# First pair of a feed-forward quantized inside the cross attention, and a table of zeros filled there instead of at the start

## The chip, the cores and the metric

The kernel runs on one core of a Trainium2 chip. A core has TensorE (PE, with its weight loads listed as PEld), VectorE (DVE), ScalarE (ACT), GpSimd (POOL) and SyncE (SP); each has its own queue of instructions, worked off in order, and meets the others through semaphores. DMAs are issued from the queues of SP, ACT and POOL. The metric is the device time of one execution in microseconds (us), the median of several runs.

## The reference

The computation is a decoder of two layers on `x` of 16 sequences x 128 tokens x 512 features, with a layernorm after every residual sum. Cut to what matters:

```python
# layer 0
x = ln(x + ssm(x))            # selective scan over 4 x 1024 tokens, 16 states per feature
x = ln(x + cross(x, ctx))     # 16 heads of 128, rope and rms norm on q and k
x = ln(x + ffn(x))
# layer 1
x = ln(x + bit_attention(x)); x = ln(x + gated_cross(x, ctx)); x = ln(x + moe(x))

def ffn(x):                   # ternary weights, 8-bit activations
    n = (x - mean(x)) / sqrt(var(x) + 1e-8)
    s = 127 / max(abs(n), -1)
    q = clip(round(s * n), -128, 127) / s
    return (silu(q @ sign(W_g).T) * (q @ sign(W_u).T)) @ sign(W_d).T
```

The mixture of experts routes each token to 8 of 64 experts. The kernel collects the rows of each group of experts in buckets in device memory, which have to hold zeros before rows are written to them.

## The kernel before, in words

Five stages run one after the other: `stage_ssm` (0 to about 623 us of the profiled span), `stage_xattn` (to about 1641), `stage_ffn` (to about 1938), `stage_attention` and `stage_moe`. The sixteen `x` tiles of 128 tokens x 512 features stay in on-chip memory throughout.

A tile scheduler orders the work. It takes the program's instructions in the order in which they are written as priorities, models their durations, and may place an instruction on its engine's queue earlier or later than it is written, as far as data and buffers allow. An instruction that is written in one stage can therefore run in another. Once compiled, each queue is fixed. A DMA goes out on one of eight lanes in turn, and its issue waits on the issuing queue until the DMA before it on that lane has landed.

*The scan stage.* Eight pairs of sequences, 16 states each, give 128 units. For each unit ACT computes decays (`h`, L234 and L236), SP loads the row `BC` broadcast to all partitions (L243), POOL multiplies (`dBx`, L245), DVE runs a scan (L254 or L258), and PE sums over states into `py` (L267). In between, a plan written by hand steps three side jobs: the projection of the next pair, the output of the last pair (L182 to L201, ending in the normalization L200), and the keys and values of a later cross attention (`keys_values`, L203 to L225), whose tiles go to device memory by DMAs that ACT issues (`x_k`, L215; `x_v`, L223). After the last state ACT copies the sums `y` (L272).

*The cross attention.* For each sequence `project` loads the transposed context `cT` (SP, L473), makes queries, keys and values (L483), and applies rope (L450 to L460) with tables of sines that `SinTables` builds on DVE (L349 to L368). Units of two heads then go through a pipeline: scores (L555), maximum (L561), exponential (L568), norm (L574, L575), transposes (L583, L586), outputs (`ao` L595, `aT` L600, `po` L606) and the sum into `x` (L609). A list `running` holds jobs that `advance` steps once for each step of the pipeline; it begins with `clear_rows` (L394 to L402), which writes 16 rows of `results` and, by 96 DMAs of 388 KB, the buckets, all from a table `zeros` in device memory. That table is filled at the very start of the program: one `x` tile is set to zero, and two POOL DMAs (L1700, L1701) copy it.

*The feed-forward.* `load_ffn_weights` loads weights and takes their signs on ACT (L659 for gate and up, L669 for down, tiles `w`). The weights share five slots of on-chip memory, so that a load or a sign waits until the slot's last reader is done. Pairs of sequences are then prepared: normalized (`xn`, L72), quantized (`qs`, `q_t`, `q_q`, L680 to L691), and transposed on PE (`ptq`, L701) into `q_T` (L703). The loop does, for each quarter `h` of the hidden features, the products `pg` and `pu` (L755), silu and product (`sg`, L758 on ACT, L759 on DVE), four transposes, a split in a high and a low part (L764, L765), and the product `po` (L769). Beside it run side jobs for the next stage, stepped from the second pair on by this line and its body:

```python
if n and h >= 2:
    next(ahead, None)
```

The jobs are the scales and ternary weights of the bit attention (`load_bit_weights`, with sums `bw_tot` at L807) and the mask of the gated attention (`load_gated_masks`: `anyk` L834, `mb` L837 and L839). The first pair is prepared before the loop, in one go:

```python
for _ in prepare(states[0]):
    pass
```

Of the kernel before, what the change touches and what calls it, by code (L numbers as in the profile page):

```python
# [10 lines left out]
F32 = mybir.dt.float32  # L11
BF16 = mybir.dt.bfloat16
# [3 lines left out]
AF = mybir.ActivationFunctionType  # L16
ALU = mybir.AluOpType
AX = mybir.AxisListType
PSUM = bass.MemoryType.PSUM

P = 128
NB = 16
D = 512
KC = D // P
NT = NB * P
MAGIC = 12582912.0
# [48 lines left out]
def stage_ssm(k):  # L75
# [6 lines left out]
    nc, tc, a = k.nc, k.tc, k.args  # L82
    NS, BQ = 16, 2
    TQ = BQ * P
    with ExitStack() as ctx:
        cst = ctx.enter_context(tc.tile_pool(name="s1c", bufs=1))
# [160 lines left out]
        def scan(u):  # L247
            st, n = units[u]
            h = st.h[n]
            hf, df = h.rearrange("p c b t -> p (c b t)"), st.dBx[n].rearrange("p c t -> p (c t)")  # L250
            Cn = st.BC[n][:, 1].unsqueeze(1).to_broadcast([P, KC, TQ])
            if n % 8 in (1, 4, 6):
                hC = wk.tile([P, KC, TQ], F32, tag="hs", name="hs")
                nc.vector.tensor_tensor_scan(hC.rearrange("p c t -> p (c t)"), hf, df, 0.0, ALU.mult, ALU.add)  # L254
                nc.gpsimd.tensor_tensor(hC, hC, Cn, ALU.mult)
            else:
                hC = wk.tile([P, KC, TQ], F32, tag="hC", name="hC", bufs=3)
                nc.vector.tensor_tensor_scan(hf, hf, df, 0.0, ALU.mult, ALU.add)  # L258
                nc.vector.tensor_tensor(hC, h.rearrange("p c b t -> p c (b t)"), Cn, ALU.mult)
            st.hC[n] = hC  # L260
# [30 lines left out]
        for u, (st, n) in enumerate(units):  # L291
            p = u // NS
            if n == 0:
                if p + 1 < NP:
                    nxt = project(states[p + 1], load_x(p + 1))
                for i in range(BQ):
                    nc.sync.dma_start(k.x[p * BQ + i], a["x"][p * BQ + i])
                if p == 2:
                    load_xattn_weights(k, 0)
            if u + 1 < len(units):  # L300
                decays(u + 1)
            if u + 2 < len(units):
                terms(u + 2)
            scan(u)
            for what in plan[n].strip("-") if u else "":
                next({"k": kv, "o": late, "n": nxt}[what], None)
            if u:
                add(u - 1)
            if u == 2:
                load_kv()  # L310
            if n == 0 and p:
                late = output(p - 1, states[p - 1].y)
# [78 lines left out]
            nc.sync.dma_start(k.wo[i], a["xa_woT"][i * 1024 : (i + 1) * 1024].rearrange("(h p) e -> p h e", p=P))  # L391


def clear_rows(k):  # L394

    for h in range(2):
        for bucket, result in zip(k.bucket[h], k.results[h]):
            k.nc.sync.dma_start(result[0:1], k.zeros[0:1, 0:D])
            for j in range(Moe.TILES):
                k.nc.sync.dma_start(bucket[j * P : (j + 1) * P], k.zeros)  # L400
                yield


def stage_xattn(k):
# [9 lines left out]
    with ExitStack() as ctx:  # L414
# [175 lines left out]
        def outputs(st, g):  # L590
# [17 lines left out]
            if g == G - 1:  # L608
                nc.vector.tensor_tensor(k.x[st.b], st.po, k.x[st.b], ALU.add)  # L609
                yield  # L610
                if st.b % 2:
                    xs = k.x[st.b - 1 : st.b + 1]
                    layernorm(k, xs, xs)
                    yield

        def advance():
            for job in list(running):
                if next(job, running) is running:
                    running.remove(job)

        units = [(b, g, i) for b in range(NB) for g in range(G) for i in range(2)]
        running = [clear_rows(k)]
        for t in range(-12, len(units) + 4):
            for lag, what in ((3, turn), (2, norm), (1, exps), (0, top), (-1, scores)):
                if not 0 <= t - lag < len(units):
                    continue
                b, g, i = units[t - lag]
                st = state[b]
                if what is scores and (g, i) == (0, 0):
                    st.b, st.sc, st.mx, st.pr, st.sm, st.pTs = b, {}, {}, {}, {}, {}  # L630
                what(st, g, i)
                if what is turn and i == 1:
                    running.append(outputs(st, g))
            b, r = divmod(t + 11, U)
            if r == 0 and b < NB:
                running.append(project(b))
            b, r = divmod(t + 15, U)
            if t == -12 or r == 0 and b > 0 and b < NB and b % 4 == 0:
                running.append(angles(max(b, 0) // 4))
            advance()  # L640
# [29 lines left out]
        k.fd.append(fd.rearrange("p (h e) -> p h e", h=8))  # L670


def quantize(k, ins, floor=None):


    nc, n = k.nc, len(ins)
    s = k.small.tile([P, n], F32, tag=f"qs{n}", name="qs")
    step = k.small.tile([P, n], F32, tag=f"qst{n}", name="qst")
    for i, x in enumerate(ins):
        nc.vector.tensor_reduce(s[:, i : i + 1], x, AX.X, ALU.max, apply_absolute_value=True)  # L680
    if floor is not None:
        nc.vector.tensor_scalar(s, s, floor, None, ALU.max)
    nc.vector.reciprocal(s, s)
    nc.vector.tensor_scalar(s, s, 127.0, None, ALU.mult)
    nc.vector.reciprocal(step, s)
    outs = []
    for i, x in enumerate(ins):
        t = k.wk.tile([P, D], F32, tag="q_t", name="q_t")
        q = k.wk.tile([P, D], BF16, tag="q_q", name="q_q")
        nc.vector.tensor_scalar(t, x, s[:, i : i + 1], MAGIC, ALU.mult, ALU.add)  # L690
        nc.scalar.activation(q, t, AF.Identity, bias=k.nmagic)  # L691
        outs.append(q)
    return outs, step


def transpose_q(k, pool, q):

    nc = k.nc
    pt = pool.tile([P, KC, P], BF16, tag="pp", name="ptq")
    for c in range(KC):  # L700
        nc.tensor.transpose(pt[:, c], q[:, c * P : (c + 1) * P], k.identb)  # L701
    qT = k.wk.tile([P, KC, P], BF16, tag="q_T", name="q_T")
    nc.scalar.copy(qT, pt)  # L703
    return qT


def stage_ffn(k):
# [2 lines left out]
    nc, tc = k.nc, k.tc  # L710
    HB = 4
    with ExitStack() as ctx:
        k.wk = wk = ctx.enter_context(tc.tile_pool(name="s3w", bufs=3))
        pg = ctx.enter_context(tc.tile_pool(name="s3g", bufs=2, space=PSUM))
        pp = ctx.enter_context(tc.tile_pool(name="s3p", bufs=2, space=PSUM))
        po_ = ctx.enter_context(tc.tile_pool(name="s3o", bufs=1, space=PSUM))
# [2 lines left out]
        ahead = chain(load_bit_weights(k, raws, po_), load_gated_masks(k, raws))  # L719

        def prepare(st):

            xn = [wk.tile([P, D], F32, tag="xn", name="xn") for _ in st.xs]
            layernorm(k, st.xs, xn, 1e-8)
            yield
            qs, st.step = quantize(k, xn)
            yield
            st.qT = []
            for q in qs:
                st.qT.append(transpose_q(k, po_, q))  # L730
                yield

        def finish(st):
            layernorm(k, st.xs, st.xs)
# [1 line left out]

        states = []
        for b0 in range(0, NB, 2):
            st = Ctx()
            st.xs = k.x[b0 : b0 + 2]  # L740
            states.append(st)
        for _ in prepare(states[0]):
            pass
        late = iter(())
        for n, sn in enumerate(states):
            nxt = prepare(states[n + 1]) if n + 1 < len(states) else iter(())
# [36 lines left out]
def load_bit_weights(k, raws, psum):  # L783
# [20 lines left out]
    views = [raw[:, :, 0:512], rawo, raw[:, :, 512:640], raw[:, :, 640:768]]  # L804
    tot = k.small.tile([P, 4], F32, tag="bw_tot", name="bw_tot", bufs=1)
    for i, w in enumerate(views):
        nc.vector.tensor_reduce(tot[:, i : i + 1], w, AX.XY, ALU.add, apply_absolute_value=True)  # L807
        yield
    pt = psum.tile([P, 4], F32, tag="pp", name="ptw")
    nc.tensor.matmul(pt, ones, tot, start=True, stop=True)  # L810
# [7 lines left out]
    outs = [wb[:, :, 0:512], wb[:, :, 768:1280], wb[:, :, 512:640], wb[:, :, 640:768]]  # L818
    for i, (w, o) in enumerate(zip(views, outs)):
        nc.vector.tensor_scalar(w, w, rsw[:, i : i + 1], MAGIC, ALU.mult, ALU.add)  # L820
        nc.vector.tensor_scalar(w, w, MAGIC, 1.0, ALU.subtract, ALU.min)
        nc.vector.tensor_scalar(o, w, -1.0, None, ALU.max)
        yield


def load_gated_masks(k, raws):


    nc, a, pool = k.nc, k.args, k.bit_pool
    m8 = raws.tile([P, NB, P], U8, name="m8")  # L830
    nc.sync.dma_start(m8, a["mask"].rearrange("b t -> (b t)").partition_broadcast(P).rearrange("p (b t) -> p b t", b=NB))
    yield
    k.gated_any = pool.tile([P, NB], F32, name="anyk")
    nc.vector.tensor_reduce(k.gated_any, m8, AX.X, ALU.max)  # L834
    yield
    k.gated_mask = mb = pool.tile([P, NB, P], BF16, name="mb")
    nc.vector.tensor_scalar(mb, m8, 1e30, -1e30, ALU.mult, ALU.add)  # L837
    yield
    nc.vector.tensor_tensor(mb, mb, k.gated_any.unsqueeze(2).to_broadcast([P, NB, P]), ALU.mult)  # L839
    yield  # L840


# [829 lines left out]
def decoder(ctx: ExitStack, tc: tile.TileContext, args):  # L1672
# [22 lines left out]
    k.zeros = dram.tile([P, Moe.ROW], F32, name="zeros")  # L1695
    k.moe, k.to_route, k.moe_ctx = None, [], ctx.enter_context(ExitStack())
    k.x = [const.tile([P, D], F32, name=f"x{b}") for b in range(NB)]
    zero = k.x[NB - 1]
    nc.gpsimd.memset(zero, 0.0)
    nc.gpsimd.dma_start(k.zeros[:, 0:D], zero)  # L1700
    nc.gpsimd.dma_start(k.zeros[:, D:], zero[:, 0 : Moe.ROW - D])  # L1701
    wctx = ctx.enter_context(ExitStack())
    wpool = wctx.enter_context(tc.tile_pool(name="weights", bufs=5, side="right"))
    k.wslot = lambda dt=F32: wpool.tile([P, 8192 if dt == BF16 else 4096], dt, tag="w", name="w")
    nc.scalar.preload_act_table_set("natural_log_exp_and_others")
    actx = ctx.enter_context(ExitStack())
    for stage in STAGES:
        if stage is stage_ffn:
            k.bit_pool = actx.enter_context(tc.tile_pool(name="bit", bufs=1))
        if stage is stage_attention:  # L1710
            wctx.close()
            k.gated_pool = actx.enter_context(tc.tile_pool(name="gated", bufs=1))
        if stage is stage_moe:
            actx.close()
        stage(k)
# [77 lines left out]
```

## Time and profile before

| what | value |
|---|---|
| median of 3 runs | 3377.56 us (3376.58 to 3380.5) |
| profiled execution | 3382.4 us |
| its span | 3380.6 us |
| mean granted clock of TensorE | 0.965 |
| PE busy | 3153.0 us, 93% |
| DVE, ACT, POOL busy | 1876.7, 1379.5, 1389.5 us |
| moved by DMA | 317.28 MB, mean 94 GB/s |

The page of the profile has the busy time of each engine, the span cut into 40 slices with the busy share of each engine in tenths, the DMA queues, and the costliest groups of instructions. In a line of a timeline stand the start, the duration, the engine, the line of the code, the operation, outputs and inputs, the number of instructions taken together, and in brackets how long the engine had been idle before and what released it. "ACTq" and "SPq" are the sequencers of these engines, which issue DMAs. Buffer numbers are left out of names. A mean over the span hides that the stages have different limits, so the stretches around the change are read one by one.

### The profile page before, as it was taken

What the parts mean: (1) busy time and instruction counts of PE and PEld (TensorE: products, weight loads), DVE (VectorE), ACT (ScalarE), POOL (GpSimd) and SP (SyncE); (2) the same over time, 40 slices, a digit from 0 to 9 for tenths busy, and PEclk for the clock granted to TensorE, in tenths of its full rate; (3) what the DMA queues carried; (4) which work ended last, traced back from release to release, by engine and by line L of the source; (5) the groups of instructions that cost most, each with busy time, mean ns of one, the idle gap of its engine ahead of it and who ended that gap; (6) DMA issues with size and microseconds to landing.
All of it is one profiled execution on the core that took longest, in us unless ns stands there. A gap on an engine that the chain in (4) does not pass through costs nothing. (4 is left out here: it accounts for less than half of the span.)

```text
span 3380.6 us, 38522 instructions
## 1 busy us (share of the span) xinstructions
PE 3153.0 (93%) x12894; PEld 1813.6 (54%) x12944; DVE 1876.7 (56%) x4202; ACT 1379.5 (41%) x3299; POOL 1389.5 (41%) x1198
## 2 busy tenths in 40 slices
PE   6888999899999999999799989998989999989998
PEld 3444444355555555555466555665655566556665
DVE  5877888456556556455576669765643232222223
ACT  4655655133333233234333379865643232112221
POOL 6967887133323333332000066325624454233331
PEclk8999999899999999999899989999999999999999
DMA  6887332200000000002200010013335665445441
GB/s 230 261 259 223 98 88 69 68 7 4 7 4 4 7 4 4 7 1 94 91 1 1 17 47 1 11 57 148 137 133 175 201 233 189 163 156 172 163 158 65
DMA packets 161553, 317.28 MB, mean 94 GB/s; under 512 B 19113, under 2 KB 82089, under 8 KB 158276
## 3 DMA queue, kind: packets, MB, share of 16 engines
q1 hardware_dynamic: 123012, 215.83, 20.8%
q0 software_dynamic: 19328, 64.56, 5.5%
q10 hardware_dynamic: 19008, 34.35, 2.7%
q8 instruction: 105, 1.72, 0.2%
q14 instruction: 100, 0.82, 0.1%
HBM read 238.80 MB, written 129.04 MB: 109 GB/s over the span
## 5 line engine op out<-in xcount | busy, mean ns | idle before, releaser
L245 POOL TENSOR_TENSOR dBx<-dtx,BC 128x1024 f32<-128x1024 f32 x128 | 301.2, 2373 | 44.8 <-DVE h L258 35.1
L1529 PE MATMUL pg<-gu,xgT 128*128 128x352 f32 x784 | 301.7, 467 | 0.0
L1529 PE MATMUL pu<-gu,xgT 128*128 128x352 f32 x784 | 299.6, 464 | 0.0
L1546 PE MATMUL y<-dn,aT 128*128 128x512 f32 x588 | 268.3, 592 | 0.0
L1533 DVE SCALAR_TENSOR_TENSOR act<-pu,row,act 128x352 f32<-128x352 f32 x98 | 57.1, 583 | 376.3 <-PE pu L1529 317.9
L575 POOL TENSOR_TENSOR pr<-pr,sm 128x512 f32<-128x512 f32 x128 | 134.7, 1053 | 289.6 <-DVE sm L574 244.2
L236 ACT ACTIVATE h<-dt,negA 128x254 f32<-128x254 f32 x512 | 239.8, 474 | 14.9 <-DVE dt L178 2.1
L1572 POOL TENSOR_TENSOR x<-got,x 128x512 f32<-128x512 f32 x120 | 152.2, 1274 | 226.4 <-DMA got<-results,gidx 225.2
L606 PE MATMUL po<-w,aT 128*128 128x512 f32 x512 | 232.2, 597 | 1.1 <-DVE aT L600 1.1
L483 PE MATMUL pq<-w,xT 128*128 128x512 f32 x512 | 228.9, 594 | 0.0
L1565 POOL DMA_INDIRECT got<-results,gidx x120 | 116.2, 968 | 268.9 <-DMA results<-yo 216.1
L460 POOL TENSOR_TENSOR m<-m,m 128x512 f32<-128x512 f32 x96 | 121.6, 1267 | 247.0 <-DVE m L455 247.0
L258 DVE TENSOR_TENSOR_SCAN h<-h,dBx 128x1024 f32<-128x1024 f32 x80 | 183.0, 2294 | 71.0 <-ACT h L236 48.7
L568 ACT ACTIVATE pr<-sc,mx,sf 128x256 f32<-128x256 f32 x256 | 142.8, 562 | 187.0 <-DVE mx L561 176.1
L267 PE MATMUL py<-hC,ident 128*128 128x512 f32 x320 | 164.6, 643 | 49.1 <-ACT y L272 49.1
L1529 PEld LDWEIGHTS pu<-gu,xgT 128*128 128x128 f32 x784 | 151.2, 193 | 85.1 <-issue 4.2
L1529 PEld LDWEIGHTS pg<-gu,xgT 128*128 128x128 f32 x784 | 144.1, 194 | 64.7 <-issue 3.0
L1532 ACT ACTIVATE act<-pg 128x352 f32<-128x352 f32 x98 | 45.5, 464 | 318.6 <-PE pg L1529 248.9
L1546 PEld LDWEIGHTS y<-dn,aT 128*128 128x128 f32 x588 | 104.1, 190 | 100.8 <-issue 94.2
L1521 ACT COPY xgT<-ptx 128x512 f32<-128x512 f32 x98 | 57.5, 587 | 233.9 <-PE ptx L375 209.6
L483 PEld LDWEIGHTS pq<-w,xT 128*128 128x128 f32 x512 | 93.5, 190 | 102.0 <-issue 99.0
L606 PEld LDWEIGHTS po<-w,aT 128*128 128x128 f32 x512 | 95.4, 191 | 96.9 <-issue 92.9
(363 smaller groups left out, 6808.3 us busy)
## 6 DMA issues: line engine op xcount, KB each, us to landing
bucket<-zeros SPq DMA_DIRECT2D x96, 388.0 KB
row<-bucket SPq DMA_DIRECT2D x90, 388.0 KB
BC<-bcd SPq DMA_DIRECT2D x128, 256.0 KB
results<-yo ACTq DMA_DIRECT2D x90, 256.0 KB
gu<-in_moe_guT SPq DMA_DIRECT2D x16, 1408.0 KB
cT<-in_ctxT SPq DMA_DIRECT2D x32, 256.0 KB
dn<-in_moe_downT SPq DMA_DIRECT2D x16, 512.0 KB
rows<-r_row SPq DMA_DIRECT2D x16, 388.0 KB
```

The source lines that it names most:

```text
L236: nc.scalar.activation(h[:, c, :, 1:], st.dt[:, c].rearrange("p (b t) -> p b t", b=BQ)[:, :, 1:], AF.Exp, scale=negA[:, c, n : n + 1])
L245: nc.gpsimd.tensor_tensor(dBx, st.dtx, BC[:, 0].unsqueeze(1).to_broadcast([P, KC, TQ]), ALU.mult)
L258: nc.vector.tensor_tensor_scan(hf, hf, df, 0.0, ALU.mult, ALU.add)
L267: nc.tensor.matmul(st.py[c], k.ident, st.hC[n][:, 2 * c : 2 * c + 2], start=n == 0, stop=n == NS - 1)
L460: nc.gpsimd.tensor_tensor(m1, m1, m2, ALU.add)
L483: nc.tensor.matmul(ps, src[:, c], w[c], start=c == 0, stop=c == KC - 1)
L568: nc.scalar.activation(pr[:, j], st.sc[g, i][:, j], AF.Exp, scale=st.sf[:, h : h + 1], bias=st.mx[g, i][:, j : j + 1], accum_out=sm[:, j : ...
L575: nc.gpsimd.tensor_tensor(pr, pr, sm.unsqueeze(2).to_broadcast([P, 2, 2 * P]), ALU.mult)
L606: nc.tensor.matmul(st.po, aT[:, j], k.wo[h // 8][:, h % 8], start=h == 0, stop=h == G * J - 1)
L1529: nc.tensor.matmul(ps, u.xT[:, c], gu[:, c, lo : lo + I], start=c == 0, stop=c == KC - 1)
L1546: self.nc.tensor.matmul(u.y, u.aT[:, c], u.w[1][:, c], start=c == 0, stop=c == 2)
L1572: nc.gpsimd.tensor_tensor(k.x[b], got, k.x[b], ALU.add)
```

## The change

Four edits go together.

1. The table of zeros is no longer filled at the start of the program. `clear_rows` takes a pool of the cross attention, sets a tile of 128 x 97 elements to zero there, and fills the table by eight DMAs on SP, each of 97 columns (388 bytes a row). The clears read that table, as before.
2. The feed-forward's first pair is prepared by a job `prepare_first` in the list `running` of the cross attention, appended four units before the last. It uses tiles of the cross attention: `xn` in the buffers `m1`, `q_t` in `m2`, `q_q` in `sq`, the transposes in the PSUM buffers `pt`; only `q_T` has buffers of its own, in a new pool `early`. Preparation itself is one generator, `prepare_ffn`, for the first pair and for the later ones.
3. The DVE instructions of the side jobs in the feed-forward are wrapped in `keep_in_program_order`, so that the scheduler doesn't move them against the instructions written around them.
4. In the scan stage, `add(u - 1)` comes ahead of the plan's step for the first state of a pair, and after it for the others.

```diff
@@ stage_ssm
             scan(u)
+            if u and not n:
+                add(u - 1)
             for what in plan[n].strip("-") if u else "":
                 next({"k": kv, "o": late, "n": nxt}[what], None)
-            if u:
+            if n:
                 add(u - 1)
@@
-def clear_rows(k):
-
+def clear_rows(k, pool):
+
+    n = Moe.ROW // 8
+    zero = pool.tile([P, n], F32, name="zero")
+    k.nc.gpsimd.memset(zero, 0.0)
+    for i in range(8):
+        k.nc.sync.dma_start(k.zeros[:, i * n : (i + 1) * n], zero)
+    yield
     for h in range(2):
         for bucket, result in zip(k.bucket[h], k.results[h]):
             k.nc.sync.dma_start(result[0:1], k.zeros[0:1, 0:D])
@@ stage_xattn
+        def prepare_first():
+
+            homes = {"xn": (wk, "m1", 4), "q_t": (wk, "m2", 2), "q_q": (wk, "sq", 2), "pt": (ppt, "pt", 2), "q_T": (k.early, "q_T0", 2)}
+            st = k.ffn_first = Ctx()
+            st.xs = k.x[0:2]
+
+            def new(what, shape, dt):
+                pool, tag, bufs = homes[what]
+                return pool.tile(shape, dt, tag=tag, name=what, bufs=bufs)
+
+            return prepare_ffn(k, st, new)
...
-        running = [clear_rows(k)]
+        running = [clear_rows(k, cst)]
...
+            if t == len(units) - 4:
+                running.append(prepare_first())
@@
-def quantize(k, ins, floor=None):
...
-def transpose_q(k, pool, q):
...
+def prepare_ffn(k, st, new):
+
+    nc = k.nc
+    xn = [new("xn", [P, D], F32) for _ in st.xs]
+    layernorm(k, st.xs, xn, 1e-8)
+    yield
+    s = k.small.tile([P, 2], F32, tag="qs2", name="qs")
+    st.step = k.small.tile([P, 2], F32, tag="qst2", name="qst")
+    for i, x in enumerate(xn):
         nc.vector.tensor_reduce(s[:, i : i + 1], x, AX.X, ALU.max, apply_absolute_value=True)
     nc.vector.reciprocal(s, s)
     nc.vector.tensor_scalar(s, s, 127.0, None, ALU.mult)
+    nc.vector.reciprocal(st.step, s)
+    qs = []
+    for i, x in enumerate(xn):
+        t = new("q_t", [P, D], F32)
+        qs.append(new("q_q", [P, D], BF16))
         nc.vector.tensor_scalar(t, x, s[:, i : i + 1], MAGIC, ALU.mult, ALU.add)
+        nc.scalar.activation(qs[i], t, AF.Identity, bias=k.nmagic)
+    yield
+    st.qT = []
+    for q in qs:
+        pt = new("pt", [P, KC, P], BF16)
+        for c in range(KC):
+            nc.tensor.transpose(pt[:, c], q[:, c * P : (c + 1) * P], k.identb)
+        st.qT.append(new("q_T", [P, KC, P], BF16))
+        nc.scalar.copy(st.qT[-1], pt)
+        yield
@@ stage_ffn
-            st = Ctx()
+            st = Ctx() if b0 else k.ffn_first
             st.xs = k.x[b0 : b0 + 2]
             states.append(st)
-        for _ in prepare(states[0]):
-            pass
@@ load_bit_weights, load_gated_masks
-        nc.vector.tensor_reduce(tot[:, i : i + 1], w, AX.XY, ALU.add, apply_absolute_value=True)
+        k.tc.keep_in_program_order(nc.vector.tensor_reduce(tot[:, i : i + 1], w, AX.XY, ALU.add, apply_absolute_value=True))
...
-    nc.vector.tensor_reduce(k.gated_any, m8, AX.X, ALU.max)
+    k.tc.keep_in_program_order(nc.vector.tensor_reduce(k.gated_any, m8, AX.X, ALU.max))
...
@@ decoder
-    zero = k.x[NB - 1]
-    nc.gpsimd.memset(zero, 0.0)
-    nc.gpsimd.dma_start(k.zeros[:, 0:D], zero)
-    nc.gpsimd.dma_start(k.zeros[:, D:], zero[:, 0 : Moe.ROW - D])
...
+        if stage is stage_xattn:
+            k.early = actx.enter_context(tc.tile_pool(name="early", bufs=1))
```

## The prediction

> **What bounds the kernel now.** I read the page first: TensorE is the busiest engine, in nearly every slice, while the DMA engines are full only in the first sixth of the span. That sixth is where the 96 large clears (37 MB) run.
>
> ```profile
> PE 3153.0 (93%) x12894; PEld 1813.6 (54%) x12944; DVE 1876.7 (56%) x4202; ACT 1379.5 (41%) x3299; POOL 1389.5 (41%) x1198
> PE   6888999899999999999799989998989999989998
> DMA  6887332200000000002200010013335665445441
> bucket<-zeros SPq DMA_DIRECT2D x96, 388.0 KB
> ```
>
> Next, the table of windows over the stretches that the change touches (columns: stretch; length; PE, PEld, DVE, ACT, POOL busy; clock; DMA share; GB/s). The cross attention (640 to 900) keeps PE busy for 255 of 260 us with idle queues; the feed-forward from 1700 is at 235.88 of 238. Between them lie 21 us in which PE does 1.2 us of work and DVE 20.8.
>
> ```profile
> 640.00:900.00 260.00, 255.25 (x829) 135.56 (x828) 153.18 (x405) 89.61 (x211) 97.39 (x107) 0.99 0.02 6
> 1641.00:1662.00 21.00, 1.21 (x9) 0.98 (x10) 20.83 (x65) 5.93 (x8) 1.26 (x4) 0.59 0.43 140
> 1662.00:1700.00 38.00, 37.68 (x175) 22.67 (x178) 17.68 (x28) 14.54 (x23) 0.00 (x0) 0.96 0.00 1
> 1700.00:1938.00 238.00, 235.88 (x1142) 145.53 (x1161) 157.90 (x428) 82.84 (x135) 0.00 (x0) 1.00 0.00 1
> ```
>
> **The scan stage, where the clears leave.** The clears are called in the cross attention, but the scheduler puts them on SP from 97 to 343 us, between the loads of BC. In the DVE timeline the first scans of the eight pairs start at 36.3, 100.4, 161.9, 239.2, 317.2, 387.3, 458.3 and 529.5 us: the pairs from the fifth on, clear of clears, take 70.2, 70.9 and 71.3 us (mean 70.8), the third and fourth 77.4 and 77.9. The ACT timeline shows why: in the third pair the store of the keys (L215) waits on ACT's own queue from 171.2 to 179.4 for a load of BC that stands behind clears. The normalization L200 behind it then runs at 179.7. In a quiet pair the store issues at once. PE's sum `py` waits for ACT's copy of `y`, behind all this: 9.78 us against 4.95.
>
> ```profile
> 170.66 0.58 ACT L214 COPY kt<-pk 128x512 f32<-128x512 f32 x1
> 179.36 0.33 ACTq L215 DMA_DIRECT2D x_k<-kt  x1
> 179.74 1.52 ACT L200 ACTIVATE x<-x,s_sh,rs_y 128x512 f32<-128x512 f32 x2 [8.50 <-DMA BC<-bcd]
> 190.66 2.08 PE L267 MATMUL py<-hC,ident 128*128 128x512 f32 x2 [9.78 <-ACT y L272]
> ...
> 396.14 0.58 ACT L214 COPY kt<-pk 128x512 f32<-128x512 f32 x1
> 396.75 0.33 ACTq L215 DMA_DIRECT2D x_k<-kt  x1
> 403.24 1.52 ACT L200 ACTIVATE x<-x,s_sh,rs_y 128x512 f32<-128x512 f32 x2 [6.52 <-DVE s_sh L198]
> 411.31 2.08 PE L267 MATMUL py<-hC,ident 128*128 128x512 f32 x2 [4.95 <-ACT y L272]
> ```
>
> The change fills the table of zeros only in the cross attention, so no clear can run earlier. The compiled order of PE, ACT, DVE and POOL in this stage stays the same; SP loses 112 clears. Gain by difference to the quiet pairs: 77.4 - 70.8 = 6.6 and 77.9 - 70.8 = 7.1. In the second pair a value copy waits 1.76 us for the key store (113.8 us); I take 2.0 with what follows it (0 to 2.5). At the start a memset and two POOL DMAs of 0.39 MB leave the queues ahead of the first matmul at 12.3 us, of some 3.5 MB queued there: 0.5 (0 to 1.3). Sum -16.2, bounds -8 (only half of the difference is the clears') to -18.
>
> **The cross attention, where the clears arrive.** SP now has eight table DMAs, 16 small clears and 96 large ones. In SP's new order the eight stand ahead of the first `cT`, each after the second waiting on the queue for an earlier load (wo, norm weights, positions) to land, so `cT` comes some 4 to 5 us later than for its present matmul at 633.4. Its result isn't needed at once: the next product `pv` started at 645.5, released by the rope on DVE, which waited for the sine tables (POOL's `tk0c`, 644.0). The cover is about 5 us after the 6 us of matmul; without it each us late is one us. I take +0.5, bounds -1 to +3.
> The table is now written in rows of 388 bytes. By the nearest rate in the trace, 246 GB/s in the window of 97 to 343, 0.39 MB take 1.6 us. The Trainium skill ("DMA: Bandwidth & Descriptors", Specifications) says that below 512 bytes a transfer misses line rate through read-modify-write; nothing in this trace isolates it. If it doubles the write, an estimate of mine from that page, everything behind is 1.6 us later: inside the cover, so +0.5 by the one, up to +2 by the other. I take the trace.
> The large clears then share SP with `cT`: 9 stand before the second, and 17, 34, 68 and 96 in all before the third to sixth. Those are needed at 672, 712, 774, 838 and 899 us; from 637 that leaves 3.9, 4.4, 4.0, 3.0 and 2.7 us for each. Between 97 and 343 us they took 246/96 = 2.56 us each beside other traffic; at 246 GB/s alone 1.6. So 0, bounds 0 to +5. No instruction leaves PE here, so no gain.
>
> **The feed-forward's start.** These are PE, ACT and DVE lines in turn:
>
> ```profile
> 1637.31 3.70 PE L606 MATMUL po<-w,aT 128*128 128x512 f32 x8 [0.78 <-DVE aT L600]
> 1659.98 0.61 PE L701 MATMUL ptq<-identb,q_q 128*128 128x128 bf16 x4 [18.97 <-ACT q_q L691]
> 1668.87 1.19 PE L769 MATMUL po<-w,hi 128*128 128x512 f32 x4
> ...
> 1641.80 3.89 ACT L669 ACTIVATE w<-w 128x1024 fp32r<-128x1024 f32 x4 [9.25 <-DMA w<-in_ff_wdT]
> 1662.49 1.28 ACT L758 ACT_TABLE_LOAD   x1
> ...
> 1648.15 2.29 DVE L807 TENSOR_REDUCE bw_tot<-l_raw 128x1 f32<-128x2048 f32 x1
> 1658.58 0.86 DVE L690 TENSOR_SCALAR q_t<-xn,qs 128x512 f32<-128x512 f32 x2
> 1665.58 0.74 DVE L759 SCALAR_TENSOR_TENSOR sg<-pu,qst,sg 128x512 f32<-128x512 f32 x1
> ```
>
> PE waits 18.97 us for the first pair's quantization, which DVE reaches late because 9.4 us of side jobs (sums of the next stage's weights: 2.29 + 0.68 + 2.28 + 0.68; mask: 2.28 + 1.22) lie in its way, and a 2.29 us one ahead of the first `sg`. In the new order the pair is quantized inside the cross attention and the side jobs stand after the twelfth `sg`.
> What is late next? ACT: the signs of the last down weights start when these landed and the last `po` is read, 1641.8, and last 3.9; then 1.28 of table load: `sg` at 1647.0, done 1647.7. DVE: `x` at 1641.05, then three statistics (2 us), the two small chains of a normalization (2.7), three scalings (1.5): 1648.3. So the product `sg` moves from 1665.6 to 1648.4: -17.2, bounds -14 to -18. PE has its first gate and up products until then.
> New in the tail of the cross attention: eight transposes (0.61 + 0.58 = 1.2 us on a full PE), some 6 us of DVE work and 2.5 of ACT at half load, for which I add 0.5: +1.7 (+1 to +4). ACT's last sign of `wu` also slips behind four exponentials, and the load of `wd` behind it by about 4 us: covered, since its signs wait until 1628.65 for `po` anyway; beyond some 9 us it would count one for one.
> On the clock: the profile grants 0.59 from 1641 to 1662, and the first four products took 1.49, 1.91, 1.19 and 1.03 us. The Trainium skill ("TensorE: Matmul & The Clock Gate", What's actually happening) halves the clock after an idle window of about 3.4 us. A wait of some 3 us for `sg` remains, so the slow stretch may only move: 0 by the trace's first order (DVE set the pace there), +1.7 by the rule. I take +0.5.
>
> **The rest of the feed-forward.** The side jobs now run in its second and third pairs, 11.7 us on a DVE that is busy 158 of 238 us. They are pinned, and a product `sg` behind one waits up to 2.3 us, with PE behind it; two halves of work lie in flight. +0.5, bounds 0 to +5. Moving `add(u - 1)` ahead changes no order: 0. Later stages keep theirs.
>
> **Sum.** -16.2 + 0.5 + 0 - 17.2 + 1.7 + 0.5 + 0.5 = -30.2. The profiled execution took 3382.4 us (span 3380.6 and 1.8 around it), so 3352.2 for one like it; it lies 4.8 above the median of the runs, and the same difference on 3377.6 gives 3347.4: 3347.
>
> **Rivals.**
> A. Only the feed-forward gains, because the long third and fourth pairs have another cause than the clears: -14, 3364. Against it: the waits name BC and land at those two pairs; for it: a shorter wait may only uncover the next. 0.11.
> B. Only the scan gains: the start of the feed-forward is held by the down weights (the slip behind the exponentials above 9 us), or the pinned jobs give back what it won: about -15, 3362. 0.10.
> C. Slower: the clears starve `cT`. PE is full here, so each us of delay counts. The decisive load is the sixth, behind 96 clears, with 2.73 us each; at p us the delay is 96 x (p - 2.73), and from 3.05 us it eats all 30. At 3.2 it is 45, net +15: 3392. For it: 2.56 measured is near; against: that was with 84 MB moved in 345 us, and here the queues are empty. 0.06.
> D. Both gains are small because the releasers named aren't what decides: 3377. 0.03.
> The rest, 0.70, is the sum, with 3337 to 3357 as its own range.
>
> **How the numbers follow.** Differences over 0.2% (6.8 us) can be told from none. Case C and some of D are slower: 0.07; same 0.03; faster 0.90. The range, 3337 to 3364, takes in the sum and A and B.
>
> **What would show it.** Right: scan starts of the third and fourth pairs some 71 us after each other; no `BC` wait at L200; first `pk` of the cross attention near 638 and `pv` still near 645 (less the scan's gain); after the last `po` of the cross attention the first `po<-w,hi` 10 us later instead of 28; the feed-forward's window at 99% PE. Wrong: a `cT` wait of PE in the cross attention, the third pair still at 77, or a wait of `sg` for side jobs.

## The result and the profile after

The changed kernel takes 3353.35 us in the median of 6 runs (3347.57 to 3355.1), against 3377.31 (3376.58 to 3382.89): 24 us less by the medians, and 0.81% or 27 us by the ratio of 0.9919 (95% interval 0.9909 to 0.9929). Its profiled execution took 3354.11 us, with a span of 3352.3: 28.3 us less than the span before.

From the page of the changed kernel: the row of DMA shares shows that the clears have moved, from the second to fourth slices to the eighth and ninth. PE's busy time is within 8 us of the 3153.0 before, in a shorter span.

```profile
PE 3160.3 (94%) x12944; PEld 1814.2 (54%) x12944; DVE 1874.6 (56%) x4202; ACT 1381.0 (41%) x3299; POOL 1390.2 (41%) x1196
PE   6899998899999999999999899998989999999998
DMA  6533332780000000002200100023345575445441
```

The table of windows of the changed kernel, with the columns as before: the clears in the cross attention (620 to 744), the stretch behind them, and the start and the rest of the feed-forward. While the clears move 305 GB/s, PE is busy for 122.17 of 124 us. The hole ahead of the feed-forward, from the last `po` to the first product of a high part, is 9.7 us long. Before, it reached from 1641.0 to 1668.9: 27.9 us.

```profile
620.00:744.00 124.00, 122.17 (x381) 63.79 (x382) 71.38 (x187) 39.41 (x93) 49.06 (x57) 0.97 0.91 305
744.00:880.00 136.00, 134.10 (x447) 71.97 (x447) 82.05 (x215) 48.71 (x116) 47.85 (x50) 1.00 0.05 16
1624.50:1634.20 9.70, 4.82 (x21) 2.49 (x19) 9.06 (x37) 7.04 (x8) 1.26 (x4) 0.84 0.89 295
1634.20:1666.00 31.80, 31.71 (x155) 19.79 (x154) 13.71 (x25) 11.14 (x18) 0.00 (x0) 1.00 0.01 3
1666.00:1904.00 238.00, 236.73 (x1161) 145.94 (x1160) 167.83 (x434) 82.71 (x135) 0.00 (x0) 1.00 0.00 1
```

The timelines of ACT and PE in the third pair of the scan stage, after: the store of the keys goes out 0.03 us after its copy, as in a quiet pair, and the normalization L200 waits for DVE and no longer for `BC`. PE waits 4.96 us for `y`.

```profile
166.56 0.58 ACT L214 COPY kt<-pk 128x512 f32<-128x512 f32 x1
167.17 0.33 ACTq L215 DMA_DIRECT2D x_k<-kt  x1
173.67 1.52 ACT L200 ACTIVATE x<-x,s_sh,rs_y 128x512 f32<-128x512 f32 x2 [6.53 <-DVE s_sh L198]
181.74 2.07 PE L267 MATMUL py<-hC,ident 128*128 128x512 f32 x2 [4.96 <-ACT y L272]
```

The first scans of the eight pairs start at 35.6, 97.6, 157.7, 229.0, 300.4, 372.0, 443.6 and 515.3 us: 71.2 and 71.5 us for the third and fourth pair. The last start came at 529.5 before, so 14.2 us are won up to here. The wait at L215 in the third pair before was for the landing of a load and not for its issue: SP had issued that load of `BC` at 170.12, it landed at 179.29, and the store went out at 179.36.

At the start of the feed-forward, after (PE, ACT and DVE in turn), PE still waits 4.88 us, now for `sg` on ACT, which stands behind the signs of the down weights and the table load:

```profile
1620.78 3.70 PE L614 MATMUL po<-w,aT 128*128 128x512 f32 x8
1631.51 1.01 PE L767 MATMUL pg<-w,q_T 128*128 128x512 bf16 x2 [4.88 <-ACT sg L770]
1634.18 1.31 PE L781 MATMUL po<-w,hi 128*128 128x512 f32 x4
...
1625.56 3.90 ACT L691 ACTIVATE w<-w 128x1024 fp32r<-128x1024 f32 x4 [9.55 <-DMA w<-in_ff_wdT]
1629.48 1.28 ACT L770 ACT_TABLE_LOAD   x1
1630.77 1.27 ACT L770 ACTIVATE sg<-pg,qst 128x512 f32<-128x512 f32 x2
...
1631.49 0.75 DVE L771 SCALAR_TENSOR_TENSOR sg<-pu,qst,sg 128x512 f32<-128x512 f32 x1 [0.40 <-ACT sg L770]
```

What the two profiles differ by, event by event, read from PE's timelines:

| event | before, us | after, us | shift | new in this stretch |
|---|---|---|---|---|
| last transposes of `x` in the scan stage | 623.24 | 607.50 | -15.7 | -15.7 |
| first keys `pk` of the cross attention | 633.36 | 621.33 | -12.0 | +3.7 |
| first queries `pq` | 656.35 | 639.92 | -16.4 | -4.4 |
| keys of the second sequence | 672.17 | 655.73 | -16.4 | 0.0 |
| end of the last `po` of the cross attention | 1641.01 | 1624.48 | -16.5 | -0.1 |
| first product with `hi` | 1668.87 | 1634.18 | -34.7 | -18.2 |
| end of the feed-forward | 1937.71 | 1904.08 | -33.6 | +1.1 |
| end of the span | 3380.6 | 3352.3 | -28.3 | +5.3 |

So 33.6 us are won up to the end of the feed-forward, and 5.3 are lost in stages that the change doesn't touch.

A shift between two profiles holds the change and the clock together. In three places the 13 profiles of this case part them.

*The cross attention.* From the first queries to the sum into `x` of the fourth sequence, a stretch in which most of the clears run after, the two kernels take the same time, with the same PE work (columns as before; 0.02 and 0.34 are the DMA shares):

```profile
656.35:960.68 304.33, 302.32 (x998) 161.89 (x997) 175.36 (x465) 104.09 (x253) 108.95 (x115) 1.00 0.02 5
639.92:944.24 304.32, 302.31 (x998) 161.91 (x997) 175.03 (x463) 104.14 (x253) 108.98 (x115) 1.00 0.34 112
```

From there to the twelfth sequence the kernel before takes 500.7 us and the changed one 498.9. The difference is the clock: before, PE is granted half of it for 3.3 us, and after it is not.

```profile
1300.20:1303.50 3.30, 3.30 (x6) 1.24 (x5) 0.78 (x2) 3.26 (x6) 0.87 (x2) 0.50 0.03 7
```

In the last two sequences it is the other way: from the sum of the fourteenth to that of the sixteenth it is 57.0 us before and 58.7 after.

```profile
1584.02 0.68 DVE L609 TENSOR_TENSOR x<-po,x 128x512 f32<-128x512 f32 x1
1641.05 0.69 DVE L609 TENSOR_TENSOR x<-po,x 128x512 f32<-128x512 f32 x1 [3.79 <-PE po L606]
1565.83 0.68 DVE L617 TENSOR_TENSOR x<-po,x 128x512 f32<-128x512 f32 x1
1624.51 0.69 DVE L617 TENSOR_TENSOR x<-po,x 128x512 f32<-128x512 f32 x1 [3.79 <-PE po L614]
```

All nine profiles of kernels with the early preparation have 58.6 or 58.7 there, and the four others 57.0. So the new work costs 1.6 us in the tail (1.7 in this pair of profiles), and the -0.1 in the table hides it behind 1.8 us that the clock took before.

*The start of the cross attention.* PE waited 2.74 us for the sine tables ahead of the values `pv` before, and doesn't after. But `pv` also ran at a granted clock of 0.53 before (645.49 to 652.04) and 1.00 after:

```profile
645.49 6.71 PE L483 MATMUL pv<-w,cT 128*128 128x512 f32 x8 [2.74 <-DVE m L455]
631.35 3.60 PE L491 MATMUL pv<-w,cT 128*128 128x512 f32 x8
```

The eight products of the first keys, 5.95 us before and 6.75 after, give 0.8 of these 3.1 us back. Without both the stretch up to the first queries would be 1.6 us longer after in place of 0.7 shorter: an estimate from these durations.

*The scan stage.* The fifth pair, which starts when the last clear of the kernel before has gone out (317.0 us), took 70.2 us before and 71.6 after:

```profile
317.12:387.31 70.19, 65.20 (x213) 33.45 (x212) 57.07 (x49) 41.64 (x97) 57.02 (x27) 0.98 0.43 120
300.41:371.96 71.55, 66.59 (x214) 33.73 (x213) 57.05 (x50) 41.66 (x97) 57.00 (x27) 0.95 0.36 89
```

In all 13 profiles the fifth to seventh pairs take 70.0 to 70.2 us at a granted clock of 0.98, and 70.8 to 71.7 at 0.95. The end of the stage, at the last transposes of `x`, lies between 620.2 and 623.2 us in the four profiles with the table filled at the start (mean 622.1), and between 604.9 and 609.7 in the nine others (mean 607.5): 14.7 us apart.

### The profile page after: what moved, and what is told of

The parts are those of the page before. It is cut to its first block, busy times and chain, and to the rows that moved or that the text cites. A ratio compares the mean times of both kernels' runs of the same rounds, so it can differ in the third digit from the quotient of the medians.

```text
span 3352.3 us, 38574 instructions
## 1 busy us (share of the span) xinstructions
PE 3160.3 (94%) x12944; PEld 1814.2 (54%) x12944; DVE 1874.6 (56%) x4202; ACT 1381.0 (41%) x3299; POOL 1390.2 (41%) x1196
## 3 DMA queue, kind: packets, MB, share of 16 engines
q1 hardware_dynamic: 124164, 216.23, 20.9%
## 4 chain that ended last, share of the span: by engine, by line
PE 64%; DVE 9%; ACT 3%; DMA 2%; issue 2%; POOL 2%; SPq 0%; ACTq 0%; POOLq 0%; DVEq 0%
PE pq L491 6%; PE y L1558 6%; PE pg L1541 6%; PE pu L1541 6%; PE po L614 6%; PE po L781 4%; PE pk L491 3%; PE ao L603 3%; PE sc L563 3%; PE pt L377 3%; PE pv L491 2%; PE ps L1142 2%; PE pg L767 2%; PE pu L767 2%; PE pT L591 1%
## 5 line engine op out<-in xcount | busy, mean ns | idle before, releaser
L1541 PE MATMUL pu<-gu,xgT 128*128 128x352 f32 x784 | 300.4, 465 | 0.0
L1558 PE MATMUL y<-dn,aT 128*128 128x512 f32 x588 | 268.3, 592 | 0.0
```

The lines of the kernel that those rows point to most:

```text
L1541: nc.tensor.matmul(ps, u.xT[:, c], gu[:, c, lo : lo + I], start=c == 0, stop=c == KC - 1)
L1558: self.nc.tensor.matmul(u.y, u.aT[:, c], u.w[1][:, c], start=c == 0, stop=c == 2)
```

## The experiments

Medians are compared with the kernel before in the same set of runs, by the ratio; the event times are from each kernel's own profile.

**The fourth edit, and the same program again.**

```diff
-            if u and not n:
-                add(u - 1)
...
-            if n:
+            if u:
                 add(u - 1)
```

> The change without its fourth edit: add(u - 1) is behind the plan's step again. Compiled, every queue has the same instructions in the same order as the changed kernel, so the theory expects no difference to it: 3353 us, within 3; if that edit does anything, some other time. The run serves a second question. In the one profile of the changed kernel the stretch from the end of the feed-forward to the end of the span takes 1448.4 us against 1443 before, though nothing was changed there. Theory P (the phase of the clock's windows decides it in each run): another value between 1440 and 1450 here, lower where the granted clock is higher. Theory Q (the change itself costs something there): 1448 again, with the same places at a lower clock.

Measured: 3353.15 us, ratio 0.9917 (0.9903 to 0.9931), as with the edit. The fourth edit does nothing. Scan stage, cross attention and feed-forward end at 609.23, 1626.18 and 1905.59 us, within 2 us of the first profile. The rest of the span takes 1448.7 us, which looks like theory Q; the second profile of the kernel before, below, takes this up.

**Each half alone.** The table of zeros moved, all else as before:

```diff
-def clear_rows(k):
+def clear_rows(k, pool):
+    zero = pool.tile([P, n], F32, name="zero")
...
-    nc.gpsimd.dma_start(k.zeros[:, 0:D], zero)
-    nc.gpsimd.dma_start(k.zeros[:, D:], zero[:, 0 : Moe.ROW - D])
```

> Only the table of zeros is moved: the kernel before, with the table filled and all clears issued in the cross attention. Theory (clears on SP hold up the key and value stores of the scan stage): third and fourth pair take about 71 us from scan to scan in place of 77, the last transpose of x in the scan stage comes at 607.5 in place of 623.2, no wait of PE for cT later on, and the whole is 16 us shorter: 3361. Rival (those pairs are long for another reason): pairs still at 77, 3377. Rival (what the scan wins, the cross attention loses to the clears): scan 16 shorter, first queries of the cross attention again at 656.

Measured: 3363.15 us, ratio 0.9953 (0.9941 to 0.9965). The pairs from the third on take 71.1, 71.4, 71.5, 71.6 and 71.6 us; the last transposes of `x` come at 605.99 us, and the distance from them to the first queries is 30.7 us (33.1 before). The clears were what held up the third and fourth pair, and the cross attention gives nothing back.

The changed kernel with the table filled at the start:

```diff
-        running = [clear_rows(k, cst)]
+        running = [clear_rows(k)]
...
+    nc.gpsimd.dma_start(k.zeros[:, 0:D], zero)
+    nc.gpsimd.dma_start(k.zeros[:, D:], zero[:, 0 : Moe.ROW - D])
```

> The changed kernel with the table of zeros filled at the start of the program as before, so that the clears run in the scan stage again; first pair and pins stay as changed. Theory (the two gains are independent and add): scan stage as before, the first product of the high parts 18 us earlier than before, from the last po of the cross attention 13.5 us in place of 31.6; whole 18 us shorter than before or somewhat less: 3360. Rival (the feed-forward only gained because the queues were free of something): no gain, 3377.

Measured: 3365.7 us, ratio 0.9962 (0.9948 to 0.9975). The scan stage ends at 622.36 us, as before, and the waits of PE there, from 60 to 345 us, are those of before again (columns: us in total, times, longest; this row read 34.2, 4, 9.8 before and 20.7, 4, 5.8 in the changed kernel from 97 to 343):

```profile
PE py L267 <- ACT y L272: 36.1, 4, 11.4
```

From the end of the last `po` to the first `hi` it is 9.2 us, 12.9 from its start as the expectation counts. The halves add up, within their intervals of about 0.13% to either side: by the ratios they win 0.47% and 0.38%, together 0.85%, and the whole change wins 0.81% to 0.83%.

**The pins.** First without them (one of six such lines is shown, here and in the next):

```diff
-        k.tc.keep_in_program_order(nc.vector.tensor_reduce(tot[:, i : i + 1], w, AX.XY, ALU.add, apply_absolute_value=True))
+        nc.vector.tensor_reduce(tot[:, i : i + 1], w, AX.XY, ALU.add, apply_absolute_value=True)
```

> The changed kernel without keep_in_program_order on the side jobs. Compiled, one sum of weights (2.29 us) then stands ahead of the first product sg on DVE, the others, with the mask, among the next ten. Theory (DVE's side jobs ahead of sg delay the start): the first sg about 2 us later and the first quarter slowed by up to 9 us of jobs in all, so 3 to 8 us slower than the changed kernel: 3356 to 3361. Rival (the early preparation alone makes the gain, PE has other work meanwhile): 3353. Rival (early jobs spare the later pairs): 3352.

Measured: 3350.18 us, ratio 0.9912 (0.9898 to 0.9926): not slower. The first `sg` waits behind one sum, and the first `hi` comes 10.5 us after the last `po` in place of 9.7; but the rest of the feed-forward takes 268.3 us in place of 269.9. That its later pairs have no side jobs would explain this, but isn't shown: with the late signs, below, the same stretch takes 268.1 us with pins and 267.8 without. The timeline of DVE of this kernel:

```profile
1630.23 2.29 DVE L819 TENSOR_REDUCE bw_tot<-l_raw 128x1 f32<-128x2048 f32 x1
1632.43 0.74 DVE L771 SCALAR_TENSOR_TENSOR sg<-pu,qst,sg 128x512 f32<-128x512 f32 x1
```

My theory of 3 to 8 us was wrong. One job of 2.29 us starts before `sg` is ready on ACT, so it delays `sg` by 0.9 us only (1632.43 against 1631.49), and the other jobs lie beside work of PE. Then the pins alone, on the kernel before:

```diff
-    nc.vector.tensor_reduce(k.gated_any, m8, AX.X, ALU.max)
+    k.tc.keep_in_program_order(nc.vector.tensor_reduce(k.gated_any, m8, AX.X, ALU.max))
```

> The kernel before with only the pins on the side jobs: clears and preparation stay where they were. Compiled, all seven jobs leave DVE's queue ahead of the first sg (9.4 us ahead of q_t and 2.3 behind it). Theory (the side jobs were most of what delayed the feed-forward): first high product about 11 us earlier than before, 3367. Rival (DVE's own preparation is long enough): 3 to 5 us only.

Measured: 3377.61 us in the median of 20 runs, ratio 0.9984 (0.9977 to 0.999). From the last `po` to the first `hi` it is 21.5 us, 6.4 less than before. PE waits 11.70 us for the first quantized tile in place of 18.97, but then the transposes and the first products come one after the other at a granted clock of 0.50 (1647.46 to 1652.68), and `sg` starts only at 1652.68:

```profile
1647.46 0.61 PE L701 MATMUL ptq<-identb,q_q 128*128 128x128 bf16 x4 [11.70 <-ACT q_q L691]
1649.12 1.91 PE L755 MATMUL pg<-w,q_T 128*128 128x512 bf16 x4
1650.83 1.91 PE L755 MATMUL pu<-w,q_T 128*128 128x512 bf16 x4
1652.68 0.69 ACT L758 ACTIVATE sg<-pg,qst 128x512 f32<-128x512 f32 x1
```

That lies between the theory's 11 and the rival's 3 to 5. So the jobs were about a third of the 18 us; the early preparation brings the rest, and with it the pins are worth nothing that these runs can show.

**Where the 5 us went that no edit touches.**

> The kernel before, unchanged, for a second profile. All five profiles of changed kernels so far take 90.7 to 91.0 us from the last transposes of the self attention's outputs to the first product with the routing weights, and 9.4 to 9.9 from the last gated output to the first expert; the one profile of before took 86.4 and 7.2. Theory P (a lucky phase of the clock in that one profile): 90 to 91 and 9 to 10 here. Theory Q (the changed kernels lose 7 us there, whatever is changed): 86.4 and 7.2 again.

Measured: 3385.5 us, one run. The stretch from the self attention's last output transposes to the first routing product takes 87.7 us, between the two theories. In the gap ahead of the first expert nothing differs: from the end of the last product `pw` of the gated attention to the first `pg` of an expert it is 9.5 us in the first profile of before, 9.6 in the second and 9.4 after, so the 7.2 of the expectation isn't found there. The pinned kernel, changed too, took 86.42, and over all 13 profiles the stretch lies between 86.4 and 91.0. The table of windows, for this stretch in the first profiles of before and after, the second of before, and the pins alone (third column from the right: granted clock):

```profile
2174.76:2261.20 86.44, 79.91 (x542) 51.94 (x543) 54.24 (x180) 62.81 (x189) 23.04 (x26) 0.98 0.21 62
2140.94:2231.78 90.84, 84.67 (x544) 54.51 (x543) 54.99 (x180) 62.96 (x189) 23.08 (x26) 0.92 0.20 59
2174.06:2261.75 87.69, 81.82 (x545) 52.47 (x543) 54.43 (x180) 62.90 (x189) 23.03 (x26) 0.96 0.20 61
2163.17:2249.59 86.42, 80.13 (x545) 51.83 (x544) 54.28 (x180) 62.77 (x189) 22.99 (x26) 0.98 0.22 62
```

The same 540 or so products take 79.9 to 84.7 us of PE, and the time follows the clock: 86.4 at 0.98, 87.7 at 0.96, 90.8 at 0.92. In full, the untouched stages take 1442.7 to 1450.7 us in the 13 profiles. They are not spread evenly: the three profiles in which neither half is changed (before, twice, and the pins alone) have 1442.7 to 1446.5 us, and of the ten others eight have 1447.7 to 1450.7, the other two 1442.9 and 1446.5. The means are 1444.0 and 1447.9. A loss of about 4 us that goes with the change is therefore not excluded. The pinned kernel's 1442.7 and its execution of 3370.26, the shortest of its 20 (to 3382.49), show how far a single execution can stand from its median.

**The remaining hole.** The changed kernel with the second half of the down weights' signs, and the last normalization of the cross attention, behind the first `sg`:

```diff
-                if st.b % 2:
+                if st.b % 2 and st.b < NB - 1:
...
+        if i:
+            k.fd_late = signs()
...
-        late = iter(())
+        late = finish(last)
...
+                    for _ in range(2):
+                        next(k.fd_late, None)
```

> The changed kernel with two things moved behind the first sg: the signs of the second half of the down weights (two after each of the first two quarters), and the last normalization of the cross attention. Theory (PE's remaining 4.9 us ahead of the feed-forward are the signs, 3.9 us, on ACT, and the normalization on DVE at the same time): the first high product comes about 4 us earlier after the last po, 3349. Rival (ACT then waits with the signs for their weights ahead of the second sg, and gives it back): 3353.

Measured: 3343.81 us, ratio 0.9888 (0.9873 to 0.9904). The hole is 5.13 us long, and PE is busy in 4.90 of it. The rest of the feed-forward gives nothing back (268.1 us). ACT's timeline of this kernel: the table load comes ahead of the signs, and two signs fit between two `sg`.

```profile
1621.53 1.28 ACT L779 ACT_TABLE_LOAD   x1 [8.62 <-PE po L614]
1622.82 0.69 ACT L779 ACTIVATE sg<-pg,qst 128x512 f32<-128x512 f32 x1
1623.41 1.99 ACT L692 ACTIVATE w<-w 128x1024 fp32r<-128x1024 f32 x2
1625.30 0.68 ACT L779 ACTIVATE sg<-pg,qst 128x512 f32<-128x512 f32 x1
```

The same without the pins:

```diff
-        k.tc.keep_in_program_order(nc.vector.tensor_reduce(tot[:, i : i + 1], w, AX.XY, ALU.add, apply_absolute_value=True))
+        nc.vector.tensor_reduce(tot[:, i : i + 1], w, AX.XY, ALU.add, apply_absolute_value=True)
```

> The kernel with late signs and late normalization, and without the pins. If the pins cost the 3 us that the run without them seemed to show: 3346; if that was chance: as with pins, 3349.

Measured: 3347.55 us, ratio 0.9896 (0.988 to 0.9912). Not faster than with pins: the 3 us of the earlier pair were chance, or too little to tell.

Only the signs late:

```diff
+        if i:
+            k.fd_late = signs()
...
+                    for _ in range(2):
+                        next(k.fd_late, None)
```

> The changed kernel with only the signs of the second half of the down weights moved behind the first sg; the last normalization stays written where it was. Compiled, the scheduler then puts most of that normalization behind the first sg by itself. Theory (ACT's signs alone held the start): first high product 5 us after the last po as with both moved (9.7 in the changed kernel), 3344 to 3349. Rival (the normalization holds it too): 8 to 9 us, 3352.

Measured: 3349.91 us, ratio 0.9903 (0.9886 to 0.9919), with the hole at 5.13 us again. The normalization needed no edit of its own, but it moved all the same: its scaling, ahead of the first `sg` in the changed kernel (first two lines), stands behind it here (last two).

```profile
1629.29 1.00 DVE L72 TENSOR_SCALAR x<-x,ln_mv,rs_y 128x512 f32<-128x512 f32 x2
1631.49 0.75 DVE L771 SCALAR_TENSOR_TENSOR sg<-pu,qst,sg 128x512 f32<-128x512 f32 x1 [0.40 <-ACT sg L770]
1627.32 0.74 DVE L778 SCALAR_TENSOR_TENSOR sg<-pu,qst,sg 128x512 f32<-128x512 f32 x1
1631.12 1.00 DVE L72 TENSOR_SCALAR x<-x,ln_mv,rs_y 128x512 f32<-128x512 f32 x2
```

So this run doesn't separate the two, and the rival stands. In the changed kernel ACT came last, but DVE waited for it only 0.40 us. In both runs that gained 4.6 us the two had moved. The median is 6 us above that of the kernel with both edits, at the same hole: in the profiles, the scan stage ended 2.4 us later here (608.71 against 606.30), and the stretch of the gated attention took 90.9 us against 88.3, neither of which the edits touch.

**The rows of 388 bytes.** The table in one write:

```diff
-    n = Moe.ROW // 8
+    n = Moe.ROW
...
-    for i in range(8):
+    for i in range(1):
```

> The changed kernel with the table of zeros written by one DMA with rows of 3104 bytes in place of eight with rows of 388. Theory (the eight issues and their waits delay the first cT, but the sine tables cover that): first keys of the cross attention 3 to 4 us earlier, first queries less than 1 us earlier, whole within noise of 3353. Rival (short rows cost the start of the cross attention): first queries 3 to 4 us earlier, 3349.

Measured: 3346.98 us, ratio 0.9897 (0.9881 to 0.9914). From the scan stage's last transposes to the first `pk` it is 11.5 us in place of 13.8, to the first queries 30.2 in place of 32.4; but the seven profiles with eight writes have 30.7 to 32.5 there, at different clocks, and the two with one write 30.2 and 30.3, so that 0.4 to 2.3 us can be put to it. The keys came 2.3 us earlier and not 3 to 4, and the queries lie between the theory and its rival. As the edit takes away issues and short rows at once, it doesn't tell which of them cost the time. SP's timeline of the changed kernel shows where the eight writes sit, with `cT` behind them:

```profile
610.04 8.15 SPq L402 DMA_DIRECT2D zeros<-zero  x8
618.24 0.43 SPq L481 DMA_DIRECT2D cT<-in_ctxT  x1
```

Both together:

```diff
+        if i:
+            k.fd_late = signs()
...
-    for i in range(8):
+    for i in range(1):
```

> Late signs and the table of zeros in one write. If both gains exist they add: 3344 with the theory on the table, 3341 with its rival.

Measured: 3344.4 us, ratio 0.9885 (0.9869 to 0.9902). With the late signs it makes the fastest version by the ratio, level with late signs and late normalization (0.9888). Both lie below the changed kernel's ratio of 0.992, by about 0.3%; which part of that the one write has is open.

## Why the prediction was right, step by step

- *Scan stage*, forecast -16.2: -15.7 at its end, 14.7 in the mean over the profiles. The difference to the quiet pairs was the right measure. Of the parts, the start brought 0.7 (forecast 0.5), the first two pairs 2.1 and 1.3 (forecast 0 and 2.0), the third and fourth 6.2 and 6.4 (6.6 and 7.1); the fifth to seventh gave back 2.5 and the eighth brought 1.5, which I had at 0. The first pair's 2.1 isn't the change's own: in the 13 profiles this pair takes either 62.0 or 64.1 us, 62.0 in the pinned kernel, which keeps its clears, and 64.1 in the changed program without its fourth edit.
- *Start of the cross attention*, forecast +0.5: -0.7 at the first queries, with luck. The first keys came 3.7 us later in their stretch, as foreseen, but the cover was not the 5 us that I read: between the first eight products and `pv` stand eight more (3.60 us), and the wait there was 2.74. That the start came out shorter is the clock's doing; at equal clock it is about 1.6 us longer, as estimated above. That is inside the range of -1 to +3.
- *Clears beside the cross attention*, forecast 0: 0.0 from the first queries to the second sequence's keys and to the fourth sequence's sum. Rival C falls: 96 clears went out from 620.2 to 743.8 us, 1.29 us each, far from the 3.05 at which it would have decided. The 2.56 that I carried over from the scan stage was misread: the large clears went out from 100.9 to 317.0 us there and not from 97 to 343, which makes 2.25 each, between other loads and waits on that queue.
- *Tail*, forecast +1.7: +1.6, in each of the nine kernels with the early preparation.
- *Start of the feed-forward*, forecast -17.2, and +0.5 for the clock: -18.2. What I named as next, signs, table load, then `sg`, is what the trace shows; only the last two come in the other order, for I had DVE last by 0.6 us (1648.3 against 1647.7) and ACT was, by 0.40. Late signs, with the normalization moved along, won 4.6 of the 4.9 us of PE's wait. Of the 9.4 us of side jobs that I put in the way of `q_t`, 1.2 (`mb`, L837, at 1661.46) stood behind it. The slow stretch of the clock moved along: behind the wait of 4.88 us the granted clock was 0.50 from 1631.51 to 1634.18, so these 2.67 us cost some 1.3 us more than at full clock, an estimate. Before it was 0.76 over the 6.8 us from the first `pg` to the first `hi`.
- *Rest of the feed-forward*, forecast +0.5: +1.1, and the run without pins took 1.6 less.
- *Untouched stages*, forecast 0: +5.3 between the two profiles. I had no term for stages whose clock differs between executions. Whether some 4 us of it go with the change is open, as said above.
- *From the profiled execution to the median*: forecast 3352.2 for a profiled execution, measured 3354.11. But I carried over that it stands 4.8 us above the median; after, it stood 0.8 above. That step, more than the sum, made 3347 out of what was 3353.4.

Rivals A and B fall with the two halves, each of which gained alone. The sum, -30.2 against -28.3 between the profiles, is close in part by luck: the terms up to the end of the feed-forward make 33.6, and 5.3 were lost where I had none. The prediction also placed the clears in the first sixth of the span; they end within the first tenth, but nothing rests on this.

One thing stays open. In each variant the ratios give 3 to 8 us less than the profiles had won up to the end of the feed-forward (27.4 against 33.6 for the change, 15.9 against 21.9 for the zeros alone, 12.8 against 20.9 for the feed-forward alone). A loss in the untouched stages would be a part of it, but not for the pins alone, where it is 5.4 against 12.0 with a short stretch at the end. Most of the timed executions have no trace, so where these us lie can't be seen. A kernel before with a mere delay ahead of the attention would tell whether the place in time matters; it wasn't tried.

## What to carry to other kernels

A large transfer that nobody needs soon can hurt through its place in a queue: the store of another engine waited for a load, and the load stood behind clears. Compare stretches of equal work with and without it, as the eight pairs here, and move it where the queues are empty and the engine that bounds doesn't use them. When a stall is removed, price the next one in line on each engine before you bank the gain: here ACT's signs took over at once, with DVE's normalization 0.4 us behind, and moving both was worth a further 4 to 5 us at that place. And when one profile is compared with another, subtract stage by stage, then look for the same stretch in every other profile: here a shift of -0.1 was +1.7 from the change and -1.8 from the clock, and only the other profiles showed it.

## What the runs showed of the hardware

The granted clock of one stretch with the same instructions varied between 0.92 and 0.98, which moved 86.4 us to 90.8; a spell of some 3.3 us at 0.50 went with 1.8 us more in the cross attention of the kernel before. Copies of 388 KB within device memory, beside a full TensorE, went out every 1.29 us, with 305 GB/s in all, and did not slow the products beside them: the stretch with most of them took 304.32 us, and 304.33 without any.
